# Placing three pairs of VectorE scalings in another part of a two-layer graph-attention loop

## The chip, the cores and the metric

The kernel runs on one core of one Trainium2 chip. The metric is the device time of one launch in microseconds. Lower is better. TensorE is the matrix engine (PE in the profile, with its weight loads shown apart as PEld), VectorE is DVE, ScalarE is ACT, GpSimd is POOL, and SyncE (SP) issues the DMAs.

## The reference

There are 64 graphs of 256 nodes with 512 features. Layer 0 is a graph attention with 8 heads of 64 units, layer 1 is a self-attention with 8 heads of 64 whose softmax is mixed with the adjacency matrix. A residual and a layer norm follow each. Everything is float32, and the node mask is all ones.

```python
def layer0(X, A, W, b, a_self, a_neigh):
    feats = einsum('bnf,hfu->bhnu', X, W)
    dense = e_self[..., :, None] + e_neigh[..., None, :]      # feats . a_self, feats . a_neigh
    dense = leaky_relu(dense, 0.2) - 1e10 * (1 - A)
    out = einsum('bhij,bhju->bhiu', softmax(dense), feats) + b
    return relu(out)                                          # heads side by side: (64, 256, 512)

def layer1(x, mask, adj, dist, W_qkv, W_out, b_out):          # called with adj = dist = A
    q, k, v = x @ W_qkv
    attn = softmax(q k^T / 8) * 0.33 + 0.33 * adj + 0.33 * exp(-dist)
    return (attn @ v) @ W_out + b_out

x = layernorm(x + layer0(x, ...))
x = layernorm(x + layer1(x, ...))
```

## The kernel before

One graph at a time passes through five stages, and the stages of different graphs run beside each other. For graph `b` they are `proj0` (features of layer 0, tiles `pf`, `v0`), `attend0` (attention of layer 0, tiles `pT`, `av0`, result in `x1`), `proj1` (q, k and v of layer 1, tiles `pq`, `qk` and `pv`, `v1`), `softmax1` (scores `pz`, exponentials `p`, row sums `pd`, reciprocals `rb`) and `attend1` (products with v in `av1`, output projection `po`).

The order of the work is written out by hand. A function `do(stage, b, step)` emits one step, and after each step `in_order` ties every new instruction to the one before it on its engine. So each engine executes in the order of the source, and the calls of `do` decide what an engine does before what. The main loop runs over `b` from 0 to 63; a pass consists of `attention0_beside_projections1(b)` and then `attention1_beside_projections0(b)`. A pass touches graph `b` in layer 0's attention, `b+1` in layer 0's projection, `b-1` in layer 1's projections and softmax, and `b-2` in layer 1's attention. A function `end` finishes the last two graphs after the loop. Steps of graphs below 0 are left out, so the steps of `attend1` for `b-2` exist in 62 passes (`b` from 2 to 63).

The projections do a two-by-two block product with seven products, `p1` to `p7`, instead of eight. They gather in three PSUM banks. Bank `chain` takes p1, p6, p7 and p4 one after the other, and ScalarE copies it out after each of the four (`COPIES`, L301). Bank `alone` takes p2. Bank `pair` takes p5, and later p3 is added onto p5. VectorE adds `alone` and `pair` to what was copied (steps `add`, `v_add` and `qk_add`, L304): 11 needs p2, 22 needs p5 and the copy after p7, 12 needs p3. Because p3 is added into the bank that step 22 reads, p3 has to wait for step 22; because p4 is added into `chain`, p4 has to wait for the copy after p7.

The step that the change moves is `weights(g)` of `attend1`, for pair `g` of heads (0 to 3). It has two VectorE instructions on the 128x1024 tile `p`:

```python
nc.vector.tensor_mul(p, p, REC[b][...])     # L750, reads rb
nc.vector.tensor_add(p, p, CT[b]...)        # L757, reads ct
```

The result is read by the matmuls of `values(g)` (L767) in `attention1_beside_projections0(b)`, where the order is values 0 and 1, scores 0 and 1, values 2 and 3, scores 2 and 3, then the output projection (L828).

Other names that are used below: `norm0` (L552 reciprocal, L554 product) takes layer 0's attention sums out of PSUM; `end` (L563) adds layer 0's residual and sums the rows; `mean` is one GpSimd instruction (L338) on those sums; `squares` is two ScalarE activations (L343) that wait for `mean`, followed by three small GpSimd instructions (L350, L353, L354); `norm` is two ScalarE activations (L358); `blocks` stores the result to DRAM and loads it again in blocks (SyncE, L636 and L114). `aT` is a VectorE transpose (L121), `far` three ScalarE activations (L384 to L387), and `shared` four to five VectorE instructions (L393 to L408).

Of the kernel before, what the change touches and what calls it, by code (L numbers as in the profile page):

```python
# [17 lines left out]
def kernel(  # L18
# [67 lines left out]
    def in_order():  # L86

        new = []
        for ins in reversed(nc.cur_bb.bb.instructions):
            if ins.name in traced:  # L90
                break
            traced.add(ins.name)
            new.append(ins)
        for ins in reversed(new):
            if ins.engine in last:
                tc.add_manual_dep(
                    ins,
                    last[ins.engine],
                    mybir.DependencyInfo(
                        mybir.DependencyClass.NoSync, mybir.DependencyReason.DATA  # L100
                    ),
                    reason="order of the source",
                )
            last[ins.engine] = ins.name
# [20 lines left out]
    def load(b):  # L125

        XB[b] = io.tile([P, C, N // B, B], FT, tag="xb", name=f"xb_{b}", bufs=1)
        load_blocks(XB[b], x[b])

    def load_adj(b):  # L130
        ADJB[b] = io.tile([P, T, N // B, B], FT, tag="adj", name=f"adj_{b}", bufs=1)
        load_blocks(ADJB[b], adj[b])
        MROW[b] = io.tile([P, N], U8, tag="mask", name=f"mask_{b}", bufs=4)
        nc.sync.dma_start(MROW[b], nodemask[b].partition_broadcast(P))

    def load_rows(b):
        X[b] = io.tile([P, T, F], FT, tag="x", name=f"x_{b}", bufs=1)
        nc.sync.dma_start(X[b], x[b].rearrange("(t p) f -> p t f", p=P))
# [718 lines left out]
    def do(stage, b, step, *args):  # L857

        if 0 <= b < NB:
            if (stage, b) not in S:  # L860
                S[stage, b] = stages[stage](b)
            S[stage, b][step](*args)
            in_order()
# [13 lines left out]
    def attention0_beside_projections1(b):  # L877


        do("attend1", b - 3, "squares")  # L880
        do("proj1", b - 1, "qk", "p1")
        do("proj1", b - 1, "qk", "p2")
        if b > 0:
            do("proj0", b, "columns")
        do("proj1", b - 1, "qk", "p6")
        for h in range(HG):
            if b > 0:
                do("proj0", b, "scaled", h)
            do("attend0", b, "weights", h)
        do("attend1", b - 3, "store")  # L890
        do("proj1", b - 1, "qk_add", 11)
        do("proj1", b - 1, "qk", "p5")
        do("proj1", b - 1, "qk", "p7")
        do("attend1", b - 2, "residual")
        do("proj1", b - 1, "qk_add", 22)
        do("attend0", b, "product", 0, 0)
        if b > 0:
            for h in range(HG, H):
                do("proj0", b, "scaled", h)
        do("proj1", b - 1, "qk", "p4")  # L900
        do("attend0", b, "product", 0, 1)
        do("attend1", b - 2, "weights", 0)
        for h in range(HG, H):
            do("attend0", b, "weights", h)
        do("attend0", b, "norm0", 0, 0)
        do("attend0", b, "norm0", 0, 1)
        do("proj1", b - 1, "qk", "p3")
        do("proj1", b - 1, "qk_add", 12)
        do("proj0", b + 1, "xT")
        if b + 2 < NB:  # L910
            load(b + 2)
        do("proj1", b - 1, "values", "p1")
        do("proj1", b - 1, "values", "p2")
        do("proj1", b - 1, "v_add", 11)
        do("attend0", b, "product", 1, 0)
        do("proj1", b - 1, "values", "p6")
        do("proj1", b - 1, "values", "p5")
        do("attend0", b, "product", 1, 1)
        do("attend0", b, "norm0", 1, 0)
        do("attend0", b, "norm0", 1, 1)  # L920
        do("attend0", b, "end")
        do("proj1", b - 1, "values", "p7")
        do("proj1", b - 1, "v_add", 22)
        do("proj0", b + 1, "product", "p1")
        do("proj1", b - 1, "values", "p4")
        do("proj0", b + 1, "product", "p6")
        do("proj1", b - 1, "values", "p3")
        do("proj1", b - 1, "v_add", 12)
        do("attend0", b, "squares")
        do("attend1", b - 2, "weights", 1)  # L930
        do("proj0", b + 1, "product", "p5")
        do("proj0", b + 1, "product", "p7")
        do("attend0", b, "norm")
        do("proj1", b, "blocks")
        if b + 1 < NB:
            load_rows(b + 1)
        do("proj0", b + 1, "add", 22)
        do("proj0", b + 1, "product", "p2")
        do("proj0", b + 1, "add", 11)
        do("proj0", b + 1, "aT")  # L940
        if b + 2 < NB:
            load_adj(b + 2)
        do("proj0", b + 1, "product", "p4")
        do("proj0", b + 1, "far")
        do("proj0", b + 1, "product", "p3")
        do("proj0", b + 1, "add", 12)
        do("attend1", b - 2, "weights", 2)
        do("attend1", b - 2, "weights", 3)

    def attention1_beside_projections0(b):  # L950

# [83 lines left out]
    for b in range(NB):  # L1035
        attention0_beside_projections1(b)
        if b == 0:
            combine_weights1()
            in_order()
        attention1_beside_projections0(b)  # L1040
# [49 lines left out]
```

## Time and profile before

| | |
|---|---|
| time, median of 3 runs (lowest to highest) | 3228.14 us (3227.4 to 3230.56) |
| the profiled run: time, span of its core | 3227.4 us, 3225.4 us |
| PE (matmuls) busy | 3129.4 us, 97% |
| PEld (weight loads) busy | 2496.2 us, 77% |
| DVE busy | 2642.8 us, 82% |
| ACT busy | 1480.9 us, 46% |
| POOL busy | 248.5 us, 8% |
| DMA engines, mean busy share of one pass | 0.40 to 0.44 |
| one pass of the loop | 48.95 us |
| in one pass: PE, DVE, ACT, POOL busy | 48.46, 41.0, 23.1, 3.87 us |
| granted TensorE clock in the passes | 1.00 |

The length of a pass is the distance between the same instruction in two neighbouring passes: the first matmuls of the q and k product start at 1589.38 us and again at 1638.34 us. Busy shares are sums over the whole span. They tell which engine is nearly always at work, not which wait is worth something; that is read from the chain of waits of one pass, below.

### The profile page before, as it was taken

What the parts mean: (1) busy time and instruction counts of PE and PEld (TensorE: products, weight loads), DVE (VectorE), ACT (ScalarE), POOL (GpSimd) and SP (SyncE); (2) the same over time, 40 slices, a digit from 0 to 9 for tenths busy, and PEclk for the clock granted to TensorE, in tenths of its full rate; (3) what the DMA queues carried; (4) which work ended last, traced back from release to release, by engine and by line L of the source; (5) the groups of instructions that cost most, each with busy time, mean ns of one, the idle gap of its engine ahead of it and who ended that gap; (6) DMA issues with size and microseconds to landing.
All of it is one profiled execution on the core that took longest, in us unless ns stands there. A gap on an engine that the chain in (4) does not pass through costs nothing.

```text
span 3225.4 us, 56184 instructions
## 1 busy us (share of the span) xinstructions
PE 3129.4 (97%) x21262; PEld 2496.2 (77%) x21262; DVE 2642.8 (82%) x5152; ACT 1480.9 (46%) x3585; POOL 248.5 (8%) x518
## 2 busy tenths in 40 slices
PE   5999999999999999999999999999999999999997
PEld 4887877877877877878878778778778778788774
DVE  6788888888888888888888888888888888888884
ACT  1444444444454454454444444444544544544442
POOL 0000000000000000000000000000000000000000
PEclk7999999999999999999999999999999999999999
DMA  7344344344344343343443443443443444434421
GB/s 158 77 111 102 97 112 105 95 116 94 102 120 93 103 119 92 104 113 90 111 103 95 113 104 96 115 95 101 120 93 103 118 93 104 112 90 111 102 79 53
DMA packets 764395, 331.89 MB, mean 103 GB/s; under 512 B 696672, under 2 KB 697440, under 8 KB 747744
## 3 DMA queue, kind: packets, MB, share of 16 engines
q1 hardware_dynamic: 764128, 328.30, 40.2%
q8 instruction: 171, 2.80, 0.4%
q14 instruction: 96, 0.79, 0.1%
HBM read 259.80 MB, written 68.16 MB: 102 GB/s over the span
## 4 chain that ended last, share of the span: by engine, by line
PE 86%; DVE 11%; DMA 1%; SPq 1%; issue 1%; ACT 0%; POOL 0%; ACTq 0%; DVEq 0%; POOLq 0%
PE pq_p L292 25%; PE po L828 14%; PE av L539 14%; PE pv_p L292 12%; PE pf_p L292 12%; DVE p L757 5%; DVE p L750 5%; PE pz L668 4%; PE av L767 2%; PE pd L697 2%; PE pr L82 1%; DVE v L304 1%; SPq L236 0%; DMA gb<-gs 0%; PE po L810 0%
## 5 line engine op out<-in xcount | busy, mean ns | idle before, releaser
L539 PEld LDWEIGHTS av<-v,pT 128*128 128x128 f32 x4096 | 493.9, 194 | 18.9 <-ACT v L485 12.4
L539 PE MATMUL av<-v,pT 128*128 128x65 f32 x4096 | 491.7, 274 | 12.1 <-ACT v L485 12.1
L292 PE MATMUL pq_p<-hC,wqk_sb 128*128 128x128 f32 x4096 | 482.5, 276 | 2.7 <-ACT qk L301 2.7
L292 PEld LDWEIGHTS pq_p<-hC,wqk_sb 128*128 128x128 f32 x4096 | 467.8, 192 | 3.5 <-ACT qk L301 3.3
L828 PE MATMUL po<-wo_sb,oT 128*128 128x512 f32 x1008 | 459.5, 599 | 0.0
L520 DVE SCALAR_TENSOR_TENSOR pT<-gb,ccol,at 128x256 f32<-128x256 f32 x1024 | 416.8, 479 | 24.0 <-ACT ccol L448 17.9
L301 ACT COPY v<-pv_p 128x256 f32<-128x256 f32 x256 | 95.7, 374 | 669.8 <-PE pv_p L292 669.8
L292 PE MATMUL pq_p<-hT,wqk_sb 128*128 128x128 f32 x3072 | 376.1, 279 | 4.9 <-DVE hT L121 4.9
L292 PEld LDWEIGHTS pq_p<-hT,wqk_sb 128*128 128x128 f32 x3072 | 355.2, 193 | 31.4 <-DVE hC L270 24.3
L828 PEld LDWEIGHTS po<-wo_sb,oT 128*128 128x128 f32 x1008 | 181.6, 190 | 204.1 <-issue 202.7
L677 ACT ACTIVATE p<-pz,hide 128x512 f32<-128x512 f32 x512 | 310.3, 689 | 31.5 <-PE pz L668 31.2
L757 DVE TENSOR_TENSOR p<-p,ct 128x1024 f32<-128x1024 f32 x256 | 313.5, 1225 | 8.7
L750 DVE TENSOR_TENSOR p<-p,rb 128x1024 f32<-128x1024 f32 x256 | 311.5, 1217 | 7.7 <-DMA rb<-rs 7.6
L343 ACT ACTIVATE junk<-x,nmean_l 128x512 bf16<-128x512 f32 x256 | 185.4, 724 | 262.8 <-POOL nmean_l L338 258.6
L767 PE MATMUL av<-p,v 128*64 128x256 f32 x2016 | 260.0, 389 | 32.8 <-DVE p L757 32.8
L485 ACT ACTIVATE v<-v 128x64 f32<-128x64 f32 x1024 | 259.8, 344 | 0.0
L292 PE MATMUL pv_p<-wv_sb,hC 128*128 128x256 f32 x1024 | 259.3, 386 | 0.3 <-DVE v L304 0.3
L668 PE MATMUL pz<-qk 64*128 64x256 f32 x2048 | 256.9, 390 | 0.6 <-ACT p L677 0.6
L292 PE MATMUL pf_p<-wf_sb,xC 128*128 128x264 f32 x1008 | 256.8, 388 | 0.5 <-ACT v L301 0.5
L767 PEld LDWEIGHTS av<-p,v 128*64 128x64 f32 x2016 | 128.1, 136 | 149.4 <-DVE p L757 61.4
L358 ACT ACTIVATE x<-x,shift_l,rstd_l 128x512 f32<-128x512 f32 x256 | 194.6, 809 | 103.4 <-POOL shift_l L354 103.4
L668 PEld LDWEIGHTS pz<-qk 64*128 64x128 f32 x2048 | 187.8, 187 | 67.8 <-issue 48.8
(107 smaller groups left out, 3792.9 us busy)
## 6 DMA issues: line engine op xcount, KB each, us to landing
gb<-gs SPq DMA_DIRECT2D x64, 1028.0 KB
rb<-rs SPq DMA_DIRECT2D x64, 1024.0 KB, 4.6
x<-in_x_dram SPq DMA_DIRECT2D x64, 512.0 KB
hs<-x SPq DMA_DIRECT2D x64, 512.0 KB
hb<-hs SPq DMA_DIRECT2D x256, 128.0 KB, 3.5
out_dram<-x SPq DMA_DIRECT2D x64, 512.0 KB, 3.0
xb<-in_x_dram SPq DMA_DIRECT2D x252, 128.0 KB, 3.8
adj<-in_adj_dram SPq DMA_DIRECT2D x256, 64.0 KB, 4.4
```

Of the source, the lines that this page charges most:

```text
L292: matmul(d, lhsT, rhs, start=(p in FIRST and i == 0), stop=(i == len(todo) - 1), skip_group_check=True,)
L343: nc.scalar.activation(junk, self.src[:, t, :], AF.Square, bias=self.nmean[:, t : t + 1], accum_out=self.rstd[:, t : t + 1],)
L358: nc.scalar.activation(self.src[:, t, :], self.src[:, t, :], AF.Identity, bias=self.shift[:, t : t + 1], scale=self.rstd[:, t : t + 1],)
L485: nc.scalar.activation(V0[b][:, t, h, :U], V0[b][:, t, h, :U], AF.Copy, scale=V0[b][:, t, h, U : U + 1],)
L520: nc.vector.scalar_tensor_tensor(pT[h][:, j, :], GB[b][:, h, :N], CCOL[b][:, j, h : h + 1], AT[b][:, j, :], op0=ALU.max, op1=ALU.mult,)
L539: matmul(av[:, k, :], pT[h][:, j, t * P : (t + 1) * P], V0[b][:, j, h, :UA], start=(j == 0), stop=(j == T - 1),)
L668: matmul(pz[:, r, j, :], QK[b][rows, g, 1, j * P : (j + 1) * P], QK[b][rows, g, 0, :], start=True, stop=True,)
L677: nc.scalar.activation(p[:, :, j, :], pz[:, :, j, :], AF.Exp, bias=hide[:, j, b : b + 1], scale=U**-0.5,)
L750: nc.vector.tensor_mul(p, p, REC[b][:, k : k + 2, g // 2, :] .unsqueeze(2) .to_broadcast([P, 2, T, N]),)
L757: nc.vector.tensor_add(p, p, CT[b].unsqueeze(1).to_broadcast([P, 2, T, N]))
L767: matmul(av[0][r * U : (r + 1) * U, g % 2, :], V1[b][:, j, 2 * g + r, :], PROBS[b][g][:, r, j, :], start=(j == 0), stop=(j == T - 1),)
L828: matmul(po, oT[:, c, t * P : (t + 1) * P], wo_sb[:, c, :], start=(c == 0), stop=(c == C - 1),)
```

## The change

Three calls are put elsewhere in `attention0_beside_projections1`. `weights(1)` stood behind `squares` and now stands behind layer 0's last product, ahead of `norm0(1, 0)`. `weights(2)` stood at the function's end and now stands behind the third product of v, ahead of step 12 of v. `weights(3)`, also at the end before, now stands ahead of the last `add` of layer 0's projection. `squares`, which has nothing on VectorE, is written ahead of step 12 of v. No instruction is added, removed or altered.

```diff
         do("attend0", b, "product", 1, 1)
+        do("attend1", b - 2, "weights", 1)
         do("attend0", b, "norm0", 1, 0)
         do("attend0", b, "norm0", 1, 1)
         do("attend0", b, "end")
...
         do("proj1", b - 1, "values", "p3")
+        do("attend0", b, "squares")
+        do("attend1", b - 2, "weights", 2)
         do("proj1", b - 1, "v_add", 12)
-        do("attend0", b, "squares")
-        do("attend1", b - 2, "weights", 1)
         do("proj0", b + 1, "product", "p5")
         do("proj0", b + 1, "product", "p7")
...
         do("proj0", b + 1, "product", "p3")
+        do("attend1", b - 2, "weights", 3)
         do("proj0", b + 1, "add", 12)
-        do("attend1", b - 2, "weights", 2)
-        do("attend1", b - 2, "weights", 3)
```

## The prediction

> **What bounds the kernel now.** I read the page's chain of work first, then the list of waits, then the chain and the timelines of one pass in the middle of the run (1540 to 1590 us; passes at 1000, 1490 and 2000 us have the same busy times to 0.01 us on PE). The chain is nearly all TensorE, with one foreign piece, VectorE's scalings L750 and L757:
>
> ```profile
> PE 86%; DVE 11%; DMA 1%; SPq 1%; issue 1%; ACT 0%; POOL 0%; ACTq 0%; DVEq 0%; POOLq 0%
> ```
>
> In order of time the same chain shows where that piece lies. TensorE ends layer 0's projection, the chain passes to VectorE for 5.3 us, and returns to TensorE at the products with v (start, length, what):
>
> ```profile
> 1568.11 4.46 PE pf_p L292 x20
> 1572.57 0.02 issue
> 1572.60 0.43 DVE v L304
> 1573.03 1.14 DVE p L750
> 1574.17 0.02 issue
> 1574.19 1.22 DVE p L757
> 1575.42 1.15 DVE p L750
> 1576.57 0.02 issue
> 1576.59 1.24 DVE p L757
> 1577.83 0.04 issue
> 1577.87 1.08 PE av L767 x8
> ```
>
> That is add 12, then weights 2 and 3 back to back, and the eight matmuls of values(3), which wait for the second one. TensorE's own timeline shows what the wait costs (start, length, instructions, idle time before and who ended it):
>
> ```profile
> 1572.49 1.95 PE L767 MATMUL av<-p,v 128*64 128x256 f32 x16
> 1574.37 2.00 PE L668 MATMUL pz<-qk 64*128 64x256 f32 x16
> 1576.30 1.08 PE L767 MATMUL av<-p,v 128*64 128x256 f32 x8
> 1577.87 1.08 PE L767 MATMUL av<-p,v 128*64 128x256 f32 x8 [0.49 <-DVE p L757]
> ```
>
> Sixteen such matmuls with nothing to wait for move the next start on by 1574.37 - 1572.49 = 1.88 us, so eight take 0.94 and values(3) could start at 1576.30 + 0.94 = 1577.24. It starts at 1577.87: 0.63 us late. The idle time shows only 0.49, since 0.14 us is the tail of a matmul that would lie under the next one. The list of waits has it in every pass, and shows where VectorE itself is idle (total us, times, longest):
>
> ```profile
> PE av L767 <- DVE p L757: 32.8, 63, 1.9
> DVE rec L552 <- PE av L539: 127.1, 64, 4.8
> DVE v L304 <- PE pv_p L292: 106.8, 64, 1.7
> ```
>
> Nothing else in that list stops TensorE in the passes. One pass is 48.95 us, PE's busy time in it 48.46, and the 0.49 is the difference. VectorE is busy for 41.0 of 48.95 us, so it isn't full: it waits 2.12 us ahead of norm0(1, 0) and 1.68 us ahead of step 12 of v, and is then late at the end.
>
> [...] the power on the row statistics (L353) took 1.69 us at 1569.84, where L757 had started at 1569.74, and 0.71 us at 1592.40, where no scaling ran. [...] L350 got through in 0.45 us, ending at 1569.75, just when L750 gave way to L757.
>
> **The change part by part.** Nothing is added or removed: 3 x 2 VectorE instructions a pass move. No DMA moves, and SyncE's order is as before. ScalarE's and GpSimd's orders are too, since between the old and the new place of `squares` there is only VectorE work. I follow VectorE through a pass. One scaling occupies the queue from its L750 to the next instruction for 1.25 + 1.14 = 2.39 us (1569.74 - 1568.49, 1570.88 - 1569.74).
>
> Weights 1. Step 11 of v starts at 1561.18, so L750 starts 0.34 later, at 1561.52, and norm0(1, 0) can follow at 1563.91. Before, it started at 1563.72, when TensorE's product was done. VectorE slips by 0.19 us through norm0, end and step 22 of v, which ends at 1566.66 instead of 1566.47. Two wait for this. The third product of v has to follow step 22 in bank `pair`; its weight load starts at 1566.86 and its matmul at 1567.08. A releaser reaches TensorE in 0.05 us (L757 ended at 1577.82, PEld started at 1577.87), so 1566.71 is in time by 0.15 us. The other is GpSimd's mean, 1566.22 before, now 1566.41, done at 1566.63; `squares` on ScalarE starts at 1567.56 behind a copy, so 0.9 us are spare. Cost between 0 and 0.25 us a pass (a slip of up to 0.4, twice what I get, less the spare 0.15); I take 0.
>
> Weights 2. They start at 1566.58 behind step 22 and end the queue's hold at 1568.97. Step 12 of v, 1568.15 before, is 0.82 us later. Nobody needs it soon: the next use of its bank is values(0) at 1572.49. The old weights 1 stood behind it until 1570.88, so from here VectorE is ahead. Steps 22 and 11 of layer 0's projection can go at about 1570.35 (the copy after p7 ends at 1570.31) and 1570.75, instead of 1570.88 and 1571.22. That helps the p3 behind step 22, whose weight load started at 1571.36, only 0.06 us after step 22 had ended.
>
> Weights 3. Behind aT, about 1571.65 to 1574.12. Add 12 slips from 1572.60 to 1574.04; its bank is next used by the output projection at 1580.8, and `bias` comes later too. So values(3) finds its input 3 us before 1577.24, and values(2), due at 1576.30, 7 us before.
>
> Sum: 0.63 us a pass on the path that sets the end, in 62 passes: 62 x 0.63 = 39 us. The scalings themselves stay, hidden under TensorE's products.
>
> Does another wait follow when TensorE comes 0.63 us earlier? Scores 2 (then 1578.25) need the first exponentials, which end by 1576.8; scores 3 (1579.2) the second, 1577.97; the projection (1580.2) the copy of values 2 and 3, 0.6 us after their end, then 1578.96. What comes after hangs on TensorE itself (L780 behind the projection, 0.15 and 0.51 us of idle ahead of it in two passes; the row statistics and the load of gb behind that), so it moves along. hT is the last input from outside: its DMA, issued by 1578.9 with 3.5 us to landing, is there at 1582.4, needed at 1586.0. VectorE keeps 7 us of idle time in a pass.
>
> So the span is 3225.4 - 39 = 3186; the median of runs, 3228.1, gives **3189 us**. The profiled run lies at 3227.4, inside the runs' 3227.4 to 3230.6.
>
> **Rivals.** Smaller gain: the wait goes over in part to the third product of v, or the tail isn't won. At 0.25 us of slip the pass gains 0.38, 24 us: 3204; with the visible idle alone, 62 x 0.49 = 30 us: 3198. For it: only 0.15 us of spare at that product. Against it: every duration in the sum is steady to some ns (L750 1215 to 1227).
>
> Slower, by GpSimd: weights 2 now run just when the mean is due. [...] it is done at 1569.3; the two squares, 1.67 us on ScalarE (1567.56 to 1569.23 before), run to 1571.0, and behind them the copy after p7 ends at 1571.4 instead of 1570.31. The p4 of layer 0's projection waits for that copy, and its weight load came at 1570.39: 1.03 us lost, 0.40 net, 62 x 0.40 = 25 us slower: 3253. Against it: the mean comes 0.17 us ahead of L750, and L350 slipped through between the two. If it gets through there, at 1567.8 + 0.22, squares slip by 0.5 us, and the copy has 0.70 spare. The rival decides from a mean done at about 1568.9, 2.5 us later than the 1566.44 of before: there the loss is 0.63.
>
> No difference: another release that I took as early holds values(3) or the scores as long (3228). The two traces of waits above speak against it.
>
> **The numbers.** About 0.2%, 6.5 us, is what a measurement of this kernel can tell from no change. Full gain 0.76 (3186 to 3193), smaller gain 0.15 (to 3215), no difference 0.03, slower 0.06. The range of 3184 to 3207 takes in the bounds of 0 to 0.25 us a pass and a few us below for the end of the run. Faster 0.91, same 0.03, slower 0.06.
>
> **What would show it.** Right: a pass of 48.3 us, no wait of L767 on L757 beyond the one at the run's end, the chain's DVE share near 0, VectorE's idle ahead of L552 nearly gone, ahead of step 12 of v gone. Wrong: PE idle at the third product of v (pv) with L304 as releaser, or at pf with ScalarE's copy as releaser and L338 far longer than 0.22 us; or a pass that is still 48.95 us.

## The result, and the profile after

The changed kernel takes 3187.8 us (median of 4 runs, 3187.4 to 3189.6), beside 3229.1 us for the kernel before: a ratio of 0.9873, 95% interval 0.9856 to 0.9890. That is 41 us or 1.3% faster, within the range given and 1 us from the predicted 3189. The span of the profiled run is 3185.4 us (3225.4 before).

The page's chain by engine, and its row for the matmuls of values (shapes and count, busy us and mean ns, idle us and releaser):

```profile
PE 85%; DVE 8%; DMA 4%; SPq 1%; issue 1%; ACT 1%; POOL 0%; ACTq 0%; DVEq 0%; POOLq 0%
...
L767 PE MATMUL av<-p,v 128*64 128x256 f32 x2016 | 245.6, 385 | 0.9 <-DVE p L757 0.9
```

The idle time of these matmuls behind L757 has gone from 32.8 us to 0.9, and what is left is the one wait in the function `end`. In one pass of the usual length the chain in order of time no longer leaves TensorE between layer 0's projection and the output projection:

```profile
1552.80 4.45 PE pf_p L292 x20
1557.25 1.88 PE av L767 x16
1559.13 1.93 PE pz L668 x16
1561.06 1.88 PE av L767 x16
1562.93 1.93 PE pz L668 x16
1564.86 3.63 PE po L828 x8
```

Values 2 and 3 are now one piece of 16 matmuls in 1.88 us. Before, they were two pieces of 8 with the scaling between. This pass takes 48.24 us; before it was 48.95.

In the list of waits (total us, times, longest), VectorE's wait ahead of L552 has shrunk from 127.1 us to 6.6. Its idle time now stands in other rows: the first below, up from 9.3 us, and two that aren't shown, ahead of L689 (up from 3.7 to 98.5 us) and ahead of L780 (from 34.7 to 89.6). One row of TensorE's weight loads, before a single wait of 0.7 us, has come up too:

```profile
DVE v L304 <- ACT v L301: 64.3, 64, 4.9
...
PEld pv_p L292 <- DVE v L304: 9.9, 13, 1.3
```

The first costs nothing: it is VectorE, now ahead of its work, waiting for the copy after p7. The second is TensorE, held at the third product of v (pv) until step 22 has read out its bank. It isn't there in every pass, only in 13; in 9 of them the matmuls themselves stop, for 4.5 us together. The pass lengths (from one start of L718 to the next) show the same. Of the 60 passes from the second to the second last, the median is 48.24 us and 12 are over 0.05 us longer than that. Two of the 12 are only shifted by 0.34 and 0.37 us, in the kernel before too, and the next pass is about as much shorter; the other ten are longer by 0.34 to 1.15 us. All 60 together are 6.8 us longer than 60 medians. This sum is called the excess below; before, it was 0.6 us.

One such pass in VectorE's timeline (start, length, then idle time and releaser), and TensorE's answer:

```profile
618.05 1.23 DVE L750 TENSOR_TENSOR p<-p,rb 128x1024 f32<-128x1024 f32 x1 [1.47 <-DMA rb<-rs]
...
628.40 1.22 DVE L750 TENSOR_TENSOR p<-p,rb 128x1024 f32<-128x1024 f32 x1
629.65 1.23 DVE L757 TENSOR_TENSOR p<-p,ct 128x1024 f32<-128x1024 f32 x1
630.79 0.17 DVE L552 RECIPROCAL rec<-av 128x4 f32<-128x4 f32 x1
...
633.11 0.42 DVE L304 TENSOR_TENSOR v<-pv_p,v 128x256 f32<-128x256 f32 x1
```

```profile
633.59 1.13 PE L292 MATMUL pv_p<-wv_sb,hC 128*128 128x256 f32 x4 [0.88 <-DVE v L304]
```

The reciprocals rb came 1.47 us too late for weights 0. From there VectorE has no idle time left until norm0 (L552 shows none), for weights 1 stand where its 2.12 us were. So the lateness reaches step 22, and TensorE loses 0.88 us of idle time plus its restart; the pass is 49.39 us long.

In another long pass it was gb, the load that L443 needs, and the chain itself runs from that load over VectorE to the third product of v (start, length):

```profile
2489.02 7.16 DMA gb<-gs
...
2512.59 1.14 DVE p L750
2513.76 1.23 DVE p L757
...
2517.30 0.35 DVE v L304
2517.69 1.13 PE pv_p L292 x4
```

From issue to use such a load takes 5.5 us in the median pass. This is where the chain's 8% of VectorE comes from. Followed pass by pass, the chain stays on TensorE in the passes of the usual length, save in some that come just ahead of a long one; in nine of the ten long ones 17 to 20 us of it are VectorE's, and most of the rest lies in the first pass, ahead of it, and at the end of the run.

### The profile page after: what moved, and what is told of

Read it like the earlier page. It is cut to its first block, busy times and chain, and to the rows that moved or that the text cites. A ratio compares the mean times of both kernels' runs of the same rounds, so it can differ in the third digit from the quotient of the medians.

```text
span 3185.4 us, 56122 instructions
## 1 busy us (share of the span) xinstructions
PE 3116.4 (98%) x21262; PEld 2502.0 (79%) x21262; DVE 2647.0 (83%) x5152; ACT 1485.6 (47%) x3585; POOL 176.2 (6%) x518
## 4 chain that ended last, share of the span: by engine, by line
PE 85%; DVE 8%; DMA 4%; SPq 1%; issue 1%; ACT 1%; POOL 0%; ACTq 0%; DVEq 0%; POOLq 0%
PE pq_p L292 21%; PE po L828 13%; PE av L539 12%; PE pf_p L292 11%; PE pv_p L292 11%; PE pz L668 7%; PE av L767 7%; DVE pT L520 2%; PE pd L697 2%; DMA gb<-gs 2%; DVE p L757 1%; DVE p L750 1%; PE pr L82 1%; DMA rb<-rs 1%; DVE qk L304 0%
## 5 line engine op out<-in xcount | busy, mean ns | idle before, releaser
L757 DVE TENSOR_TENSOR p<-p,ct 128x1024 f32<-128x1024 f32 x256 | 313.5, 1225 | 8.8
L750 DVE TENSOR_TENSOR p<-p,rb 128x1024 f32<-128x1024 f32 x256 | 309.2, 1208 | 9.2 <-DMA rb<-rs 9.0
L689 DVE SCALAR_TENSOR_TENSOR both<-p 128x512 f32<-128x512 f32 x256 | 176.6, 691 | 98.7 <-ACT p L677 98.5
L767 PE MATMUL av<-p,v 128*64 128x256 f32 x2016 | 245.6, 385 | 0.9 <-DVE p L757 0.9
L292 PEld LDWEIGHTS pf_p<-wf_sb,xC 128*128 128x128 f32 x1008 | 191.9, 191 | 33.4 <-ACT v L301 1.3
```

Source lines behind the costliest of these rows:

```text
L292: matmul(d, lhsT, rhs, start=(p in FIRST and i == 0), stop=(i == len(todo) - 1), skip_group_check=True,)
L689: nc.vector.scalar_tensor_tensor(both[g], p[:, :, 0, :], TINY, p[:, :, 1, :], op0=ALU.add, op1=ALU.add)
L750: nc.vector.tensor_mul(p, p, REC[b][:, k : k + 2, g // 2, :] .unsqueeze(2) .to_broadcast([P, 2, T, N]),)
L757: nc.vector.tensor_add(p, p, CT[b].unsqueeze(1).to_broadcast([P, 2, T, N]))
L767: matmul(av[0][r * U : (r + 1) * U, g % 2, :], V1[b][:, j, 2 * g + r, :], PROBS[b][g][:, r, j, :], start=(j == 0), stop=(j == T - 1),)
```

## The experiments

The theory that I tested (A): the gain is TensorE's restart at values(3) (the idle time there and what the stop costs around it) and nothing else, and what was lost again comes from VectorE's idle time, which had absorbed late loads. Its rivals: filling VectorE's idle time is what counts (B), the long passes have another cause (C), VectorE's total work counts (D). Each time below stands beside the kernel before on the same chip, whose medians were 3229.7 us (e1 to e4), 3229.9 (e5 to e7) and 3228.6 (e8 to e10). What lies ahead of the first pass takes from 120.0 to 124.2 us in the twelve profiles, so differences of 1 or 2 us between single runs say little; the lengths of passes say more.

**e1: weights 1 moved alone.**

```diff
+        do("attend1", b - 2, "weights", 1)
         do("attend0", b, "norm0", 1, 0)
...
-        do("attend1", b - 2, "weights", 1)
         do("proj0", b + 1, "product", "p5")
```

> One part of the change alone: weights 1 ahead of norm0, weights 2 and 3 left at the end of the function. Theory A (the gain is nothing but TensorE's restart at values(3), 0.71 us a pass, and only what makes weights 3 end earlier counts): add 12 still waits for the third product of layer 0's projection and weights 2 and 3 follow it, so the pass stays 48.95 us; about 3228 us, or 2 to 5 us more, since late loads of gb and rb now reach the third product of v. Rival B (what counts is that VectorE's idle time is filled, whichever scaling fills it): a third of the gain, about 3215 us.

Measured: 3235.8 us, ratio 1.0022 (1.0014 to 1.0030): slower by 6 us. TensorE's timeline of a pass has the old wait unchanged:

```profile
1584.13 1.08 PE L767 MATMUL av<-p,v 128*64 128x256 f32 x8
1585.71 1.08 PE L767 MATMUL av<-p,v 128*64 128x256 f32 x8 [0.50 <-DVE p L757]
```

The median pass is 48.95 us, and the 60 passes have 5.9 us of excess, against 0.6 in the kernel before. So this part wins nothing in an ordinary pass: add 12 still waits for TensorE, and weights 2 and 3 follow it. It does bring the long passes. B falls. The loss is 1 us more than the most that was expected. The span of its profiled run is 8.1 us longer than before the change, and in it the first pass takes 54.83 us instead of 50.12, the last 44.57 instead of 46.15. Why the first is so long is open.

**e2: weights 2 and 3 ahead of add 12, weights 1 left where it was.**

```diff
         do("proj0", b + 1, "product", "p3")
-        do("proj0", b + 1, "add", 12)
         do("attend1", b - 2, "weights", 2)
         do("attend1", b - 2, "weights", 3)
+        do("proj0", b + 1, "add", 12)
```

> The other part alone: weights 2 and 3 ahead of add 12 of layer 0's projection, weights 1 where it was before (behind step 12 of v). VectorE keeps its idle time of about 2.1 us ahead of norm0 and 1.7 us ahead of step 12 of v. Theory A: weights 3 end at about 1577.0 in the old pass where values(3) can start at 1577.24, so the whole 0.71 us a pass is won, and the late loads are absorbed as before: 3184 to 3186 us, a little under the change. Rival B: at most two thirds of the gain, about 3200 us.

Measured: 3186.3 us, ratio 0.9868 (0.9853 to 0.9883). The waits of its passes (180 to 3040 us):

```profile
DVE rec L552 <- PE av L539: 113.9, 59, 2.1
...
PEld av L767 <- DVE p L757: 9.2, 59, 0.2
```

The page's chain by engine:

```profile
PE 95%; DMA 2%; DVE 1%; SPq 1%; ACT 0%; issue 0%; POOL 0%; ACTq 0%; DVEq 0%; POOLq 0%
```

VectorE has its idle time back, and the matmuls of values wait in no row of PE's own, only 0.16 us a pass in the weight loads, which is hidden. The median pass is 48.24 us, the excess 0.8. Moving one step past two scalings wins what the change wins in an ordinary pass.

**e3: as e2, with weights 1 ahead of step 12 of v.**

```diff
         do("proj1", b - 1, "values", "p3")
+        do("attend0", b, "squares")
+        do("attend1", b - 2, "weights", 1)
         do("proj1", b - 1, "v_add", 12)
-        do("attend0", b, "squares")
-        do("attend1", b - 2, "weights", 1)
```

> As the run before it, and weights 1 ahead of step 12 of v, so in the idle time of 1.7 us there, not ahead of norm0. Theory A: a pass of 48.24 us throughout, TensorE never waiting for step 22 of v, 3184 to 3186 us; weights 3 are done 0.7 us ahead of values(3). Rival C (the passes over 48.24 us of the change come of something else than VectorE's lost idle time, such as the loads themselves or the clock): they stay, and the time is that of the change, about 3188 us.

Measured: 3183.1 us, ratio 0.9857 (0.9842 to 0.9872); again as e10, 3185.2, ratio 0.9862 (0.9845 to 0.9878). TensorE doesn't wait for step 22. The excess is 2.0 us in the profile of e3 and 0.3 in that of e10; what there is comes almost all in passes where gb was some 1.7 us late or more (see below).

**e4: the change again, on the chip of e1 to e3.**

> The change itself, on the same chip as the three above, for comparison. 3187 to 3190 us, with some ten passes of 48.6 to 49.4 us among those of 48.24, in each of which gb or rb landed over 1 us late.

Measured: 3188.5 us, ratio 0.9875 (0.9858 to 0.9891), excess 5.9 us. The runs of e3 (3180.5 to 3185.5) all lie below those of e4 (3186.8 to 3191.8). Those of e2 (3185.9 to 3187.7) overlap with them: e2 saves some 5 us of excess and loses nearly 3 again in the last pass (see e8).

**Late loads, counted.** In each profile I took the start of L443, which waits for gb, within its pass, less the median of that over the passes; for rb, VectorE's idle time ahead of L750. Loads over 0.3 us late come in every kernel: 13 passes of the kernel before, 14 of the change, 17 of e2, 14 of e3. What a late one does differs (some of the passes in which gb was over 1 us late):

| gb late by (us) | pass longer by (us) |
|---|---|
| kernel before: 1.44, 1.54, 1.65, 1.77 | 0.00, 0.00, 0.08, 0.20 |
| change: 1.20, 1.30, 1.48, 1.62, 1.74 | 0.34, 0.44, 0.62, 0.76, 0.87 |
| e2: 1.26, 1.38, 1.67, 2.04 | 0.00, 0.00, 0.12, 0.48 |

The change lets through all but 0.86 us of each (1.20 - 0.34, 1.74 - 0.87), the others all but some 1.6. With rb the change lets through all but 0.32 us (VectorE waited 1.25 us and the pass was 0.93 longer, 1.47 and 1.15), where a wait of 1.23 us in the kernel before and one of 1.88 in e2 cost nothing. C falls: the loads are as late in all of them, and the order without the idle time ahead of norm0 pays for much more of the lateness. The idle time ahead of step 12 of v, which e3 fills, isn't needed for that.

**e5 and e6: 0.34 us more of VectorE work a pass.** A left factor of layer 0's projection is computed a second time, to the same values, in the kernel before (e5) and in the changed one (e6).

```diff
             left_factors(xC, xT)
+            nc.vector.tensor_sub(xC[:, 3], xT[:, k2, n1], xC[:, 1])
```

> The kernel before with one more VectorE instruction a pass: the last left factor of layer 0's projection (L271, 128x256, 0.42 us, 0.34 us from start to start) is computed a second time, to the same values, ahead of step 11 of v. VectorE then reaches its idle time ahead of norm0 0.34 us later. Theory A: the idle 2.12 us take it in, nothing changes at values(3): 3227 to 3231 us. Rival D (VectorE's total work counts): 62 x 0.34 = 21 us more, about 3250.

> The same extra instruction in the changed kernel. Theory A: there the idle time ahead of norm0 is gone and only about 0.17 us are spare between step 22 of v and the third product of v, so each pass loses 0.34 - 0.17 = 0.17 us and the late loads count in full: 3188 + 11 = 3199 us, a few more or less; TensorE waits for L304 at pv in every pass. Rival D: 21 us more, 3209. If VectorE still had spare time there: 3188.

Measured: e5 3228.5 us, ratio 0.9997 (0.9989 to 1.0006), no change. e6 3204.2 us, ratio 0.9922 (0.9908 to 0.9937), some 16 us above the change, and 5 above the expected 3199. The waits of e6's passes:

```profile
PEld pv_p L292 <- DVE v L304: 28.1, 59, 1.8
```

Its median pass is 48.41 us: 0.17 more than 48.24, as expected to the hundredth (60 x 0.17 = 10 us). The excess rose to 9.6 us, 3 to 4 over that of the change. Together that accounts for the profiled run, 3201.5 us, the fastest of the four; for the others there is no profile. D falls, since the same 0.34 us are free in one order and not in the other.

**e7: the change with step 22 of v ahead of `end`.**

```diff
-        do("attend0", b, "end")
         do("proj1", b - 1, "values", "p7")
         do("proj1", b - 1, "v_add", 22)
+        do("attend0", b, "end")
```

> The change with step 22 of v put ahead of the residual and row sums of layer 0 (end), so that it ends about 0.9 to 1.2 us earlier and the third product of v has some 1.2 us spare instead of 0.17. Theory A: the late loads of gb and rb no longer stop TensorE there, though the row sums come 0.4 us later and may hold the copy after p7 in the latest passes: 3184 to 3187 us. Rival C: about 3188 us, as the change.

Measured: 3189.1 us, ratio 0.9878 (0.9861 to 0.9894): no better than the change, so the expectation missed. TensorE no longer waits for step 22, but in the passes with a late load it waits elsewhere:

```profile
PEld pf_p L292 <- ACT v L301: 4.1, 9, 0.5
```

The row sums come later, with them GpSimd's mean and the squares on ScalarE, and behind these the copy after p7 that p4 needs. And the mean, which the change does in 0.22 us, takes 1.13 us here, in all 62 passes:

```profile
1549.88 1.13 POOL L338 TENSOR_SCALAR nmean_l<-sums_l 128x2 f32<-128x2 f32 x1 [22.36 <-DVE x L563]
```

Weights 2 now follow the row sums at once: L750 started at 1549.71, ahead of the mean, and the mean ended at 1551.01, just when L750 had given way to L757 (1550.96). The excess fell to 3.4 us, but the last pass, 43.10 us in the change, took 46.65; how much of either is due to the longer mean I did not test apart from the order.

**e8 and e9: the last pass by itself.** That last pass (b = 63) has no projection of layer 0 left, so it is short of TensorE work. It takes 46.15 us before, 43.10 in the change, 45.97 in e2 and 44.17 in e3. In the chains of e2 and of the change through it stand the same GpSimd instructions, with different lengths. In e2:

```profile
3094.51 1.06 POOL rstd_l L350
...
3095.64 1.70 POOL rstd_l L353
...
3099.54 4.19 DMA hs<-x
```

In the change:

```profile
3098.69 0.67 POOL rstd_l L350
...
3099.43 0.72 POOL rstd_l L353
...
3102.40 2.78 DMA hs<-x
```

The two GpSimd instructions account for 1.37 us and the store for 1.41, together nearly the 2.87 us between the passes. Why the store takes longer in e2 is open. e8 is e2, e9 is e3, each with the order of the change when b = 63 (the edit of e8 against e2 is shown):

```diff
+        if b == NB - 1:
+            do("attend1", b - 2, "weights", 1)
         do("attend0", b, "norm0", 1, 0)
...
+        if b == NB - 1:
+            do("attend1", b - 2, "weights", 2)
         do("proj1", b - 1, "v_add", 12)
...
-        do("attend1", b - 2, "weights", 1)
+        if b < NB - 1:
+            do("attend1", b - 2, "weights", 1)
...
-        do("attend1", b - 2, "weights", 2)
+        if b < NB - 1:
+            do("attend1", b - 2, "weights", 2)
         do("attend1", b - 2, "weights", 3)
         do("proj0", b + 1, "add", 12)
```

> In the passes up to b = 62 the order of e2 (weights 1 where it was before, weights 2 and 3 ahead of add 12), in the last pass alone the order of the change. Theory A (the change loses some 5 us in late passes through VectorE's lost idle time, but wins 3 us in the last pass, where layer 0's projection is missing and VectorE holds TensorE): passes of 48.24 us almost throughout, the last one 43.1 instead of 45.97 us; about 3183 us, 3 below e2 and 5 below the change. If the last pass owes its length to something else: 3186, as e2.

> In the passes up to b = 62 the order of e3 (weights 1 ahead of step 12 of v, weights 2 and 3 ahead of add 12), in the last pass alone the order of the change. Theory A: 1 us below e3 (a last pass of 43.1 instead of 44.17 us), about 3182 us; not to be told from e8.

> e3 again, on the same chip as the two above. About 3183 us, the last pass 44.2 us.

Measured: e8 3183.4 us, ratio 0.9858 (0.9844 to 0.9873); e9 3181.8 us (3181.1 to 3182.9), ratio 0.9854 (0.9839 to 0.9869). The last pass is 43.09 us in e8 and 43.03 in e9. So the order in that one pass makes its length. e9 has the lowest median of all, 6 us below the change, though by the ratios the intervals overlap; e8 and e9 can't be told apart.

## Why the prediction was right, and where it was off

**The step on the path.** Right. The wait of values(3) for weights 3 was the only one that stopped TensorE in an ordinary pass, and it is gone. The gain a pass was mis-sized: 0.63 us forecast, 48.95 - 48.24 = 0.71 measured. I reckoned up to the start of values(3), as if its eight matmuls took 0.94 us from there. Before, they took 1578.88 - 1577.87 = 1.01 us, by the starts of values(3) and of scores 2 in TensorE's timeline. So 0.07 us more than the idle time and the tail came back.

**The sum.** 39 us forecast, 40.0 in the spans. That it agrees so well is in part luck, since terms that I had missed nearly cancel: 60 x 0.71 = 42.6 us, less 6.8 - 0.6 = 6.2 us for the late loads, and 3.05 us for the last pass, which I had entered like any other. That makes 39.5; the rest lies in the first pass, the start and the end.

**Weights 1.** The slip was forecast at 0.19 us. It was 0.19 at norm0 (2.73 us behind the start of step 11, before 2.54) and 0.17 at step 22 (5.04 behind that start, before 4.87). The spare time of 0.15 us at the third product of v was real too: e6 gives 0.34 - 0.17 = 0.17. That norm0 is held back behind a moved scaling, as forecast, the timeline above shows: L552 starts at 630.79 directly behind L757, without a wait of its own. What failed is the cost of 0 drawn from them. I argued that every duration in the sum was steady, and that holds for VectorE's instructions (L750 1180 to 1226 ns in the change, L757 1224 to 1227), but not for the landing of gb and rb (1.0 to 2.2 us late in 6 to 10 of the 60 passes). The rival of a smaller gain named the right place (the third product of v) with the wrong cause, and the sign of being wrong that was given for it, PE idle at pv with L304 as releaser, came in 9 passes (in the last it had been there before). The sign of being right that failed is a chain with VectorE's share near 0: it is 8%, from the late passes, and 1% in e2. By e1 weights 1 ahead of norm0 are worth nothing in an ordinary pass and cost 6 us over the run; what they can win lies in the last pass (44.57 us in e1, before 46.15).

**Weights 2 and 3.** Right. Step 12 of v starts 2.73 us behind step 22, before 2.10; with the slip of 0.17 that is 0.80 us later (0.82 forecast), and nobody waits for it. Weights 3 end at 1558.93, 3.0 us before values(3) could start, as forecast.

**The slower rival.** That the scalings would hold up GpSimd's mean until they end was an estimate of mine, from the 1.69 us of L353 beside L757. It did not come true here: the mean is as short as before. The row of L338 (count, shortest, median and longest ns):

```profile
L338 POOL TENSOR_SCALAR nmean_l<-sums_l x128: 218/218/221, 52.3 to 3176.8; 128x2 f32<-128x2 f32 x128
```

The danger was real all the same: in e7, where the scalings begin just ahead of the mean, the mean takes 1.13 us. The power L353 shows the like: in the kernel before it takes 1.69 us all the 63 times that it starts while L757 runs, and 0.71 us the other 65 times. That the two fall together is all that the traces show of it. In the change one L353 of the 128 starts so and takes 1.69 us, and POOL's busy time is down from 248.5 to 176.2 us. In an ordinary pass that is worth nothing: e2 has the long L353 in 63 of 128 too, and passes of 48.24 us. In the last pass it is part of what the two chains above differ by; that the scalings' place is the cause there I infer from the lengths, 1.70 and 0.72 us, and did not test apart from the order. It isn't all of the 3.05 us between the kernel before and the change: in the kernel before, the chain through the last pass runs over the scalings and TensorE, which stood idle 1.90 us for L757, and e3, with a power of 0.71 us, still has a last pass of 44.17.

## What to carry to other kernels

Idle time of an engine that isn't the bottleneck can be the buffer that takes in late loads: in the passes listed above, gb 1.44 to 1.77 us late cost 0.00 to 0.20 us with VectorE's 2.12 us of idle time ahead of norm0, and gb 1.20 to 1.74 us late cost 0.34 to 0.87 without it. Before filling it, look in the passes of the trace for how late the loads upstream come at worst, not in the median. When an engine waits at one point of a loop, look for the shortest move that takes that point out of the way: here one short step behind two long ones (e2) gave the ordinary pass its whole gain, and left the idle time where it was of use.

## What was not expected of the hardware

Loads of gb (1028 KB) and rb (1024 KB) come 1.0 to 2.2 us late in 6 to 10 of the 60 passes. Often these are the same passes in different kernels and on different chips. In nine profiles (before, after, e2, e3, e4, e7 to e10) gb was late by 1.3 to 2.1 us every time in the pass counted as 52 (the first start of L718 begins pass 0), and in most of them in those counted as 15, 18, 44 and 49. In the profiles of before, the change and e2 most of these loads of gb are issued on time and are long on the way (6.7 to 7.6 us from issue to use, in the median pass 5.5); in the pass counted as 44 the issue itself comes 1.0 to 1.3 us late. Why it is those passes is open.

A stop of TensorE, the one at values(3) in the kernel before, cost more than its idle time shows: 0.49 us idle, 0.14 us of a matmul's tail laid bare, and 0.07 us in the matmuls after it.
